# Between two attention steps: one ScalarE pass moved ahead of three projections, and block 0's products moved into an earlier period

## The chip, the cores and the metric

The kernel runs on one core of a Trainium2 chip. The metric is device time in microseconds (us) of one execution; the median of several runs is what counts. Five engines work side by side, each through its own queue in order: TensorE (PE, with its weight loads PEld), VectorE (DVE), ScalarE (ACT), GpSimd (POOL) and SyncE (SP). They meet only where one waits for another's result.

## The reference

The reference is a graph network of two layers on 2708 nodes with 256 features. Cut to what matters here:

```python
# layer 0
x = layernorm(x + relu(concat([x, adj @ x], 1) @ weight + bias))
# layer 1
R = (adj + eye(N)) / rowsum(adj + eye(N))
for n in range(2):
    q = Xa @ W1.T @ W2.T
    k = Xa @ W3.T
    probs = softmax(q @ k.T)                 # N x N
    keep = the largest probs of each row, until their sum reaches 0.9
    A = probs * keep / rowsum(probs * keep)
    Xf = R @ Xf
    Xa = A @ Xa
    Z = Z + Xf @ U1[n].T + Xa @ U2[n].T
x = layernorm(x + layernorm(x + Z))          # inner one with gain and bias
```

In each of the two steps the N x N attention is thinned in every row to the largest probabilities that hold 90% of the mass ("top-p"). `adj` has about eight entries other than zero in a row, so `R @` works on gathered rows.

## The kernel before

The 2708 rows are cut into 22 blocks of 128 (the last one, `EDGE`, has 20). All data are float32. A matmul shows as two records in the profile, a transpose as one.

Ahead of the place of interest, the kernel computes layer 0, and then step 1 of the attention block by block. At the end of a block's step 1, the result `xaT_all` (tag "V" in SBUF) is projected to the keys and queries of step 2 and, two blocks at a time, to `ya`, the right-hand side of step 2's products. `ya_pair()` does one such y pair: four matmuls into an accumulator `acc` (one of two PSUM buffers), and a copy by ScalarE (L675, for the last pair two copies L678). There are eleven pairs. The first eight run among the last instructions of step 1; the last three in a loop of their own, `while y_pairs: ya_pair()`.

Step 2 is written out by hand as a sequence of periods `per` = 0 to 23, each of six groups `g` (NG = 6). There is no scheduler: the order in which the source issues instructions is the order of each engine's queue. In a steady period four blocks are in work at once:

- block `per + 2`: TensorE makes its logits in three parts (L507, one PSUM tile `lg`, a single buffer); VectorE takes the shift from the first part (`shift`, L841); ScalarE makes the exponentials of each part (`exps2`, L844 and L848). The first part of the next block's logits is made in the last group of a period.
- block `per + 1`: ScalarE tries two levels over the whole block (`try_act`, parts 0 to 3: passes L965 and L968 of 2708 columns, and small instructions, the last of them L978 to L981 in `next_level`). The passes need an output that nobody reads, `scr`.
- block `per`: VectorE takes the last level (`last_level`, from L1002 on), makes a copy `low` of what lies below the level (`below_level`, L1022), and 20 candidates (L1029).
- block `per - 1`: VectorE sorts the candidates, finds the threshold, marks (L1082) and masks the block (`mask`, L1087). `vector_slots` is the order of the last two, six slots a period.
- block `per - 2` (`t_mul`): TensorE transposes it in six groups of four 128 x 128 tiles (`turn`, L527, PSUM tile `tr` of two buffers), ScalarE copies each group to SBUF (`wT`, two buffers, L530), and TensorE multiplies it with `ya` into an accumulator (`products`, L564), one group behind the transposes.

Beside this runs the R chain, `R @` for two right-hand sides: per block eight products ("units", `r_units`, L749) of gathered rows `yg` (POOL's indirect DMAs, L719, seven for a block, two buffers) and stored matrix tiles (SP's queue). When the eight units of a block have run, VectorE scales and adds (`r_out`, L777) two groups later. The table `units` says how many units TensorE does in each period; `first` = 16 come ahead of period 0.

The first three blocks of step 2 cannot take that form, so they have a start of their own. VectorE does both trial levels of block 0's search, except for one sum, which ScalarE makes: `try_dve(b0, 0)`, `try_dve(b0, 1)` (pass L992) on VectorE and `try_act(b0, 1, 0)` with `next_level(b0, 1)` on ScalarE. `vector_slots` has a short form for block 0 in period 1: it is sorted, marked and masked in the first four groups; block 1's last level follows in the last two.

Where tiles lie decides what may start: `tile1` (tag "x1") holds `low` and `w`, and is free once `x1` is no longer read. `tile2` (tag "V") holds the fifth buffer of the ring of blocks and `scr`; it is free once the last y pair has read `xaT_all`. POOL clears the edge of that fifth buffer (L956).

Of the kernel before, what the change touches and what calls it, by code (L numbers as in the profile page):

```python
# [9 lines left out]
FP = mybir.dt.float32  # L10
# [10 lines left out]
P = 128  # L21
# [19 lines left out]
CW, CC = 128, 7  # L41
# [107 lines left out]
def fast_path(ctx, tc, c, flags, fint, xT_d, x_d, w0_d, b0_d, w1_d, w2_d, w3_d, u1_d, u2_d, g_d, b_d):  # L149
    nc = tc.nc  # L150
    N, D, DA, NB, DC, KH, CHS, rows = c.N, c.D, c.DA, c.NB, c.DC, c.KH, c.CHS, c.rows
    ident = c.ident
    adj_d, out_d, x1_d, za_d = c.adj_d, c.out_d, c.x1_d, c.za_d
    NW = SEG * NS
    NF = flags.shape[1]

    big = ctx.enter_context(tc.tile_pool(name="big", bufs=1))
# [27 lines left out]
    b0 = es[1][:, :D]  # L185
# [44 lines left out]
    EDGE = NB - 1  # L230
# [66 lines left out]
    class Lists:  # L297
# [11 lines left out]
        def turn(self):  # L309
            n = self.n  # L310
            parts = names[:, self.a:self.b, :].rearrange("p m (s j) -> p (m s) j", j=3)
            tr = ps_tr()
            for j in range(3):
                nc.tensor.transpose(tr[:n, j, :], parts[:, :, j], ident)
            nc.scalar.copy(self.row[:n].rearrange("q (j p) -> q j p", j=3), tr[:n, :3, :])
# [72 lines left out]
    for t in range(NB):  # L388
        p = rows(t)
# [57 lines left out]
    for m in range(NB):  # L447
        p = rows(m)
# [50 lines left out]
    def logits(s, t, i):  # L499


        p = rows(t)
        lg = ps_lg()
        cs = CHS[2 * i:2 * i + 2]
        for h, (a, b) in enumerate(cs):
            o = slice(DA * h, DA * h + DA)
            nc.tensor.matmul(lg[:p, h, :b - a], lhsT=q[o, t * P:t * P + p], rhs=keys[s][o, i, :b - a],  # L507
                             start=True, stop=True)
        a, b = cs[0][0], cs[-1][1]
        return lg.rearrange("p h n -> p (h n)")[:p, :b - a], a, b  # L510
# [42 lines left out]
    def products(keep):  # L553

        if len(before) > keep:
            p, ks, wT, y, acc = before.pop(0)
            for k in ks:
                kw = rows(k)
                if p < P:
                    o = EW * (k % 4)  # L560
                    nc.tensor.matmul(acc[o:o + p, :D], lhsT=wT[:kw, k % 4, :p], rhs=y[:kw, k, :],
                                     start=k < 4, stop=k >= NB - 4)
                    continue
                nc.tensor.matmul(acc[:p, :D], lhsT=wT[:kw, k % 4, :p], rhs=y[:kw, k, :],  # L564
                                 start=k == 0, stop=k == NB - 1)
# [96 lines left out]
    def ya_pair():  # L662


        if not y_pairs:
            return
        t0 = y_pairs.pop(0)
        pz = ps_acc().rearrange("p (s d) -> p s d", d=D)
        for s in range(2):
            p, at = rows(t0 + s), (t0 + s) * P  # L670
            for j in range(DC):
                nc.tensor.matmul(pz[:p, s, :], lhsT=xaT_all[:, j, at:at + p], rhs=c.u2[:, j, 1, :],  # L672
                                 start=j == 0, stop=j == DC - 1)
        if rows(t0 + 1) == P:
            nc.scalar.copy(ya[:, t0:t0 + 2, :], pz)  # L675
            return
        for s in range(2):
            nc.scalar.copy(ya[:rows(t0 + s), t0 + s, :], pz[:rows(t0 + s), s, :])  # L678
# [129 lines left out]
    def e2(t):  # L808
        return ring[t % 5]
# [40 lines left out]
    def begin_search(b):  # L850

        nc.vector.tensor_reduce(b.z, b.all[:b.p, :NL], AX.X, ALU.add)
        yield
        nc.vector.reciprocal(b.rz, b.z)
        nc.vector.tensor_scalar(b.nz, b.z, -1.0, None, op0=ALU.mult)
        yield
        nc.vector.tensor_scalar(b.l0, b.roots, b.roots, b.rz, op0=ALU.mult, op1=ALU.mult)

    def run_all(steps):
        for _ in steps:  # L860
            pass
# [84 lines left out]
    for t in range(3):  # L946
        exps2(blocks[t], 2, *logits(1, t, 2))
        ya_pair()
    while y_pairs:
        ya_pair()  # L950

    tile1 = big.tile([P, 2 * NW], FP, tag="x1", name="w")
    low = tile1[:, :NW]
    w = tile1[:, NW:]
    tile2 = big.tile([P, 2 * NW], FP, tag="V", name="e4")
    nc.gpsimd.memset(tile2[:, N:NW], 0.0)  # L956
    ring.append(tile2[:, :NW])
    scr = tile2[:, NW:]

    def try_act(b, k, part):  # L960


        e = e2(b.t)[:b.p, :N]
        if part == 0:
            nc.scalar.activation(scr[:b.p, :N], e, AF.Relu, bias=b.nz, scale=b.l[k], accum_out=b.relu)  # L965
            return
        if part == 1:
            nc.scalar.activation(scr[:b.p, :N], e, AF.Sign, bias=b.nz, scale=b.l[k], accum_out=b.sign)  # L968
            return
        if part == 2:  # L970
            nc.scalar.activation(b.n, b.sign, AF.Identity, bias=halfn[:b.p], scale=0.5)
            return
        nc.scalar.activation(b.u[k], b.relu, AF.Identity, bias=b.n, scale=b.rz)
        next_level(b, k)

    def next_level(b, k):
        keep, slope, down = STEPS[k]
        nc.scalar.activation(b.kept, b.l[k], AF.Copy, scale=keep + TOP_P * slope, bias=-down)  # L978
        nc.scalar.activation((b.l1, b.l2)[k], b.u[k], AF.Identity, bias=b.kept, scale=-slope)
        if k:  # L980
            nc.scalar.activation(b.few, b.l1, AF.Copy, scale=TOP_P, bias=-FEW)  # L981
# [6 lines left out]
    def try_dve(b, k):  # L988

        e = e2(b.t)[:b.p, :N]  # L990
        level(b, b.l[k])
        nc.vector.scalar_tensor_tensor(w[:b.p, :N], e, b.d, e, op0=ALU.is_ge, op1=ALU.mult, accum_out=b.m)  # L992
        nc.vector.tensor_scalar(b.u[k], b.m, b.rz, b.l[k], op0=ALU.mult, op1=ALU.mult)
        if k == 0:
            keep, slope, down = STEPS[0]
            nc.vector.tensor_scalar(b.kept, b.l0, keep + TOP_P * slope, -down, op0=ALU.mult, op1=ALU.add)
            nc.vector.scalar_tensor_tensor(b.l1, b.u0, -slope, b.kept, op0=ALU.mult, op1=ALU.add)
# [251 lines left out]
    accs = {}  # L1249
# [1 line left out]

    each = NB * (CC + 1)
    first = 2 * (CC + 1)
    units = {0: CC + 1, 1: CC + 1}
    rest = each - first - sum(units.values())
    units.update({p: rest * (p - 1) // 8 - rest * (p - 2) // 8 for p in range(2, 10)})
    units.update({p: each * (p - 10) // 11 - each * (p - 11) // 11 for p in range(11, 22)})
    assert first + sum(units.values()) == 2 * each

# [1 line left out]
    b0, b1, b2 = (blocks[t] for t in range(3))  # L1261
    run_all(begin_search(b0))
    try_dve(b0, 0)
    run_all(begin_search(b1))
    try_dve(b0, 1)
    run_all(begin_search(b2))
    lg = logits(1, 3, 0)
    r_units(first)
    try_act(b0, 1, 0)
    next_level(b0, 1)  # L1270
    for per in range(NB + 2):
        if per == NB + 1:
            tail.append(True)
        n_r = units.get(per, 0)
        b_act = blocks.get(per + 1)
        t_mul = per - 2 if per > 1 else None
        if t_mul is not None:
            accs[t_mul] = ps_acc(t_mul)
        b_exp = None
        if per and per + 2 < NB:  # L1280
            b_exp = blocks[per + 2] = Block(per + 2)
        vector = vector_slots(blocks.get(per), blocks.get(per - 1), begin_search(b_exp) if b_exp else None)
        for g in range(NG):
            n = n_r * (g + 1) // NG - n_r * g // NG
            now = later.pop(0)
            later.append([])
            if g == 0:
                if b_exp:
                    shift(b_exp, lg[0])
                r_units(n)  # L1290
            if t_mul == EDGE:
                if g == 0:
                    products(0)
                    edge_product(ya, accs[EDGE], e2(EDGE))
            elif t_mul is not None:
                turn(t_mul, g, ya, accs[t_mul], e2(t_mul))
            if b_exp and g == 3:
                lg = logits(1, b_exp.t, 2)
            if g == NG - 1 and 3 < per + 3 < NB:
                lg = logits(1, per + 3, 0)  # L1300
            if g:
                r_units(n)
            if b_exp and g == 1:
                lg = logits(1, b_exp.t, 1)
            if t_mul is not None and t_mul != EDGE:
                products(1)
            if b_exp and g in (0, 1, 3):
                exps2(b_exp, (g + 1) // 2, *lg)
            if b_act:
                for k, part in {0: ((0, 0),), 1: ((0, 1), (0, 2), (0, 3)), 2: ((1, 0),), 3: ((1, 1), (1, 2), (1, 3))}.get(g, ()):  # L1310
                    try_act(b_act, k, part)
            next(vector)
            if g == 0:
                final_slot(0)
                if t_mul:
                    t = t_mul - 1
                    base = za_load(t)
                    later[0].append(lambda t=t, base=base: arrive(t, base, accs.pop(t), ras.pop(t)[:rows(t)]))
            for f in now:
                f()  # L1320
            if g and (per < NB + 1 or g < NG - 1):
                final_slot(g)
# [407 lines left out]
```

## Time and profile before

| | |
|---|---|
| median of 3 runs | 1325.51 us (1323.46 to 1327.99) |
| profiled execution | 1323.33 us, of which the span is 1321.6 us |
| TensorE (PE) | 1237.4 us busy, 94% |
| VectorE (DVE) | 1002.0 us busy, 76% |
| ScalarE (ACT) | 753.3 us busy, 57% |
| GpSimd (POOL) | 634.7 us busy, 48% |
| mean granted TensorE clock | 0.977 |
| last y pair's copy ends, step 2 begins | about 754 us into the span |

Busy time is a mean over stages with different limits. A row of a timeline gives the start in us from the start of the span, the length in us, the engine, the line and operation, output and inputs, and in brackets how long the engine had been idle before it and what ended that. A row of a table of stretches gives the stretch, its length, the busy time of each engine with the number of instructions, the granted clock, the share of the DMA engines and GB/s.

### The profile page before, as it was taken

How to read it: one execution, taken by the hardware profiler on the slowest of the kernel's cores; microseconds unless marked ns; L12 is line 12 of the kernel's file. 1: busy time of each engine (PE TensorE's matmuls, PEld its weight loads, DVE VectorE, ACT ScalarE, POOL GpSimd, SP SyncE). 2: the span in 40 equal slices, each digit the busy share in tenths (PEclk: the TensorE clock that was granted, in tenths of full speed). 3: DMA queues.
4: the chain of work that ended last, by engine and by line, in shares of the span. 5: the costliest groups of instructions: out<-in, count | busy, mean ns of one | idle time of the engine just before them, and what ended most of it. 6: DMA issues, size and time to landing. Idle time of an engine off the chain costs nothing.

```text
span 1321.6 us, 18910 instructions
## 1 busy us (share of the span) xinstructions
PE 1237.4 (94%) x5764; PEld 894.5 (68%) x5764; DVE 1002.0 (76%) x3420; ACT 753.3 (57%) x1338; POOL 634.7 (48%) x594
## 2 busy tenths in 40 slices
PE   8999999979899999999999969999999989998985
PEld 6877877833477777777775647777756766666763
DVE  2545555865999998877751399898897999899996
ACT  2010111025465556566564498878888899989931
POOL 1000000005275532677554187887847767787850
PEclk9999999989899999999998979999999999999998
DMA  7455544523222210223232155556545445544541
GB/s 191 163 173 168 167 153 142 171 67 123 92 77 82 70 62 10 76 91 99 76 77 86 55 172 179 177 178 184 172 118 159 148 128 166 173 148 146 166 108 38
DMA packets 101994, 166.28 MB, mean 126 GB/s; under 512 B 17394, under 2 KB 74358, under 8 KB 101882
## 3 DMA queue, kind: packets, MB, share of 16 engines
q1 hardware_dynamic: 75596, 108.91, 25.4%
q0 software_dynamic: 20544, 51.17, 14.1%
q10 hardware_dynamic: 5742, 4.89, 1.3%
q8 instruction: 48, 0.79, 0.2%
q14 instruction: 64, 0.52, 0.1%
HBM read 130.87 MB, written 34.03 MB: 125 GB/s over the span
## 4 chain that ended last, share of the span: by engine, by line
PE 70%; ACT 15%; DVE 11%; issue 3%; DMA 0%; ACTq 0%; DVEq 0%
PE acc L564 23%; PE acc L257 16%; PE lg L507 8%; PE tr L527 6%; PE misc L749 5%; ACT e L965 4%; ACT e L844 3%; ACT e L968 2%; DVE e L1087 2%; PE acc L651 2%; PE acc L462 2%; PE misc L426 2%; PE misc L392 2%; ACT e L848 2%; PE acc L672 2%
## 5 line engine op out<-in xcount | busy, mean ns | idle before, releaser
L530 ACT COPY wT<-tr 128x512 f32<-128x512 f32 (+2 forms) x258 | 131.8, 518 | 217.6 <-PE tr L527 215.9
L564 PE MATMUL acc<-ya,wT 128*128 128x256 f32 (+1 forms) x924 | 234.9, 394 | 11.4 <-ACT wT L530 11.0
L564 PE MATMUL acc<-x,wT 128*128 128x256 f32 (+1 forms) x924 | 230.5, 388 | 0.0
L719 POOL DMA_INDIRECT yg<-v_d,ix x154 | 195.0, 1266 | 64.6 <-issue 25.1
L564 PEld LDWEIGHTS acc<-ya,wT 128*128 128x128 f32 (+1 forms) x924 | 171.4, 194 | 66.0 <-issue 23.1
L719 POOL DMA_INDIRECT yg<-yf_d,ix x154 | 190.7, 1238 | 48.3 <-issue 24.3
L564 PEld LDWEIGHTS acc<-x,wT 128*128 128x128 f32 (+1 forms) x924 | 165.2, 189 | 71.0 <-issue 37.3
L257 PE MATMUL acc<-y,adj_t 128*128 128x257 f32 (+1 forms) x924 | 208.4, 381 | 0.0
L257 PEld LDWEIGHTS acc<-y,adj_t 128*128 128x128 f32 (+1 forms) x924 | 171.8, 189 | 32.7 <-issue 8.9
L367 POOL DMA_INDIRECT adj_t<-in_adj,ix x154 | 165.6, 1076 | 51.8 <-issue 41.7
L749 PE MATMUL misc<-yg,adj_t 128*128 128x256 f32 (+1 forms) x704 | 180.6, 392 | 5.9 <-DMA yg<-yf_d,ix 4.3
L507 PE MATMUL lg<-k,q 64*128 64x512 f32 (+3 forms) x528 | 152.4, 605 | 29.7 <-ACT e L848 22.3
L749 PEld LDWEIGHTS misc<-yg,adj_t 128*128 128x128 f32 (+1 forms) x704 | 125.2, 190 | 54.3 <-issue 23.1
L527 PE MATMUL tr<-ident,e 128*128 128x128 f32 (+2 forms) x946 | 147.9, 275 | 2.5 <-DVE e L1087 2.5
L527 PEld LDWEIGHTS tr<-ident,e 128*128 128x128 f32 (+2 forms) x946 | 114.1, 140 | 41.9 <-issue 18.8
L334 POOL DMA_DIRECT2D part_d<-e x1 | 0.6, 573 | 285.3 <-DVE e L333 285.3
L439 ACT COPY x1T<-tr 128x256 f32<-128x256 f32 (+1 forms) x22 | 8.0, 364 | 186.7 <-PE tr L438 186.7
L965 ACT ACTIVATE e<-e,st 128x2708 f32<-128x2708 f32 (+1 forms) x43 | 113.5, 2640 | 0.1
L968 ACT ACTIVATE e<-e,st 128x2708 f32<-128x2708 f32 (+1 forms) x42 | 111.0, 2642 | 0.1
L570 DVE MAX8 cand<-e 128x8 f32<-128x170 f32 (+1 forms) x352 | 87.2, 317 | 27.4 <-ACT e L514 27.4
L1029 DVE MAX8 cand<-w 128x8 f32<-128x136 f32 (+1 forms) x440 | 106.1, 285 | 0.0
L507 PEld LDWEIGHTS lg<-k,q 64*128 64x128 f32 (+1 forms) x528 | 39.5, 184 | 63.5 <-ACT e L848 30.1
(239 smaller groups left out, 1780.8 us busy)
## 6 DMA issues: line engine op xcount, KB each, us to landing
adj_t<-in_adj SPq DMA_DIRECT2D x44, 704.0 KB
adj_t<-adjc_d SPq DMA_DIRECT2D x44, 448.0 KB
adjc_d<-adj_t SPq DMA_DIRECT2D x22, 256.0 KB
base<-za_d SPq DMA_DIRECT2D x41, 128.0 KB
adjc_d<-adj_t SPq DMA_DIRECT2D x22, 192.0 KB
xt<-in_x ACTq DMA_DIRECT2D x21, 128.0 KB
x_d<-x SPq DMA_DIRECT2D x21, 128.0 KB
x1b_d<-xb SPq DMA_DIRECT2D x21, 128.0 KB
```

The source lines that it names most:

```text
L257: nc.tensor.matmul(acc[:p, :n], lhsT=halves[k // KH][:kw, k % KH, :p], rhs=y[:kw, k, :n], start=k == 0, stop=stop and k == NB - 1)
L367: nc.gpsimd.indirect_dma_start(out=a[:CW, i, :], out_offset=None, in_=adj_rows, in_offset=bass.IndirectOffsetOnAxis(ap=ix[:CW, m, i:i + 1] ...
L507: nc.tensor.matmul(lg[:p, h, :b - a], lhsT=q[o, t * P:t * P + p], rhs=keys[s][o, i, :b - a], start=True, stop=True)
L527: nc.tensor.transpose(tr[:kw, k % 4, :p], e[:p, k * P:k * P + kw], ident[:p, :p])
L530: nc.scalar.copy(wT[:, :full, :p], tr[:, :full, :p])
L564: nc.tensor.matmul(acc[:p, :D], lhsT=wT[:kw, k % 4, :p], rhs=y[:kw, k, :], start=k == 0, stop=k == NB - 1)
L570: nc.vector.max(dst[:p, i * 8:(i + 1) * 8], src[:p, i * step:i * step + w])
L719: nc.gpsimd.indirect_dma_start(out=y[:CW, i, :], out_offset=None, in_=rows_d, in_offset=bass.IndirectOffsetOnAxis(ap=ix[:CW, m, i:i + 1], ...
L749: nc.tensor.matmul(acc[:p, :D], lhsT=a[:kw, k, :p], rhs=y[:kw, k, :], start=k == 0, stop=k == CC)
L965: nc.scalar.activation(scr[:b.p, :N], e, AF.Relu, bias=b.nz, scale=b.l[k], accum_out=b.relu)
L968: nc.scalar.activation(scr[:b.p, :N], e, AF.Sign, bias=b.nz, scale=b.l[k], accum_out=b.sign)
L1029: nc.vector.max(b.cand[:p, 8 * i:8 * i + 8], low[:p, SEG2 * i:SEG2 * (i + 1)])
```

## The change

Two things are done, in one diff.

First, `try_act(b0, 1, 0)`, ScalarE's pass over block 0, is issued right after VectorE's first trial and ahead of the last three y pairs. As `tile2` isn't there yet at that place, its unread output goes to `low` (`spill_room`); `tile2` is made after the pairs, and later passes write there as before. `next_level(b0, 1)` comes right after VectorE's second trial.

Second, block 0's transposes and products move from period 2 to the last two groups of period 1, three `turn`s in each, with `products(1)` after each `turn`. Period 2 has none then; the table of R units is rewritten: 20 units in period 2, and what is left is spread over periods 3 to 9 (17 or 18 each) instead of 18 in each of periods 2 to 9. The output of block 0's attention is taken in period 3 as before.

```diff
-    while y_pairs:
-        ya_pair()
 
     tile1 = big.tile([P, 2 * NW], FP, tag="x1", name="w")
     low = tile1[:, :NW]
     w = tile1[:, NW:]
-    tile2 = big.tile([P, 2 * NW], FP, tag="V", name="e4")
-    nc.gpsimd.memset(tile2[:, N:NW], 0.0)
-    ring.append(tile2[:, :NW])
-    scr = tile2[:, NW:]
+    spill_room = [low]
 
     def try_act(b, k, part):
         e = e2(b.t)[:b.p, :N]
+        scr = spill_room[0]
...
-    units = {0: CC + 1, 1: CC + 1}
+    units = {0: CC + 1, 1: CC + 1, 2: 20}
     rest = each - first - sum(units.values())
-    units.update({p: rest * (p - 1) // 8 - rest * (p - 2) // 8 for p in range(2, 10)})
+    units.update({p: rest * (p - 2) // 7 - rest * (p - 3) // 7 for p in range(3, 10)})
...
     run_all(begin_search(b0))
     try_dve(b0, 0)
+    try_act(b0, 1, 0)
+    while y_pairs:
+        ya_pair()
     run_all(begin_search(b1))
     try_dve(b0, 1)
+    next_level(b0, 1)
     run_all(begin_search(b2))
+    tile2 = big.tile([P, 2 * NW], FP, tag="V", name="e4")
+    nc.gpsimd.memset(tile2[:, N:NW], 0.0)
+    ring.append(tile2[:, :NW])
+    spill_room[0] = tile2[:, NW:]
     lg = logits(1, 3, 0)
     r_units(first)
-    try_act(b0, 1, 0)
-    next_level(b0, 1)
     for per in range(NB + 2):
...
-        t_mul = per - 2 if per > 1 else None
+        t_mul = 0 if per == 1 else per - 2 if per > 2 else None
...
-            elif t_mul is not None:
+            elif t_mul:
                 turn(t_mul, g, ya, accs[t_mul], e2(t_mul))
             if b_exp and g == 3:
                 lg = logits(1, b_exp.t, 2)
+            if t_mul == 0 and g > 3:
+                for i in range(3):
+                    turn(0, 3 * (g - 4) + i, ya, accs[0], e2(0))
+                    products(1)
             if g == NG - 1 and 3 < per + 3 < NB:
                 lg = logits(1, per + 3, 0)
             if g:
                 r_units(n)
...
-            if t_mul is not None and t_mul != EDGE:
+            if t_mul and t_mul != EDGE:
                 products(1)
```

## The prediction

> **What bounds the kernel now.** I read the page first (shares, then the chain that ended last), then a table of stretches around the seam between the steps, then the timeline of that seam. The page:
>
> ```profile
> PE 1237.4 (94%) x5764; PEld 894.5 (68%) x5764; DVE 1002.0 (76%) x3420; ACT 753.3 (57%) x1338; POOL 634.7 (48%) x594
> ...
> PE 70%; ACT 15%; DVE 11%; issue 3%; DMA 0%; ACTq 0%; DVEq 0%
> ```
>
> TensorE is busy 94% of 1321.6 us and carries 70% of the chain. So only stretches where it is not full can be filled. The table of stretches (us, then busy time of PE, PEld, DVE, ACT, POOL, the granted clock, DMA) shows them:
>
> ```profile
> 754.00:762.00 8.00, 7.89 (x36) 6.00 (x32) 4.28 (x9) 7.93 (x10) 5.40 (x5) 1.00 0.42 120
> 762.00:770.00 8.00, 3.41 (x11) 2.05 (x12) 7.72 (x36) 7.79 (x11) 6.18 (x7) 0.92 0.82 254
> 770.00:778.00 8.00, 7.69 (x22) 4.28 (x21) 7.69 (x27) 7.90 (x14) 5.86 (x8) 0.65 0.57 159
> 778.00:784.60 6.60, 1.51 (x6) 0.68 (x4) 6.43 (x10) 6.47 (x11) 5.99 (x3) 0.83 0.37 131
> 784.60:790.20 5.60, 5.52 (x15) 3.39 (x16) 5.53 (x31) 3.82 (x8) 4.38 (x5) 0.59 0.30 88
> ...
> 814.30:838.45 24.15, 23.84 (x115) 17.97 (x114) 21.04 (x78) 19.92 (x33) 19.28 (x16) 1.00 0.55 169
> ```
>
> From 762 to 784.6 VectorE and ScalarE are full, while TensorE works 3.41 of 8, 7.69 of 8 (at 0.65 of its clock) and 1.51 of 6.6 us. From 814.3 it works 23.84 of 24.15 us in each period of step 2: from there TensorE sets the pace. The seam ends when block 1's transposes (the first work of period 3) start, at 814.29. The timeline of all engines (start, length, instruction, idle time ahead and its releaser) for the start of the seam:
>
> ```profile
> 748.48 0.59 ACT L675 COPY ya<-acc 128x512 f32<-128x512 f32 x1 [1.00 <-PE acc L672]
> 754.30 2.65 ACT L965 ACTIVATE e<-e,st 128x2708 f32<-128x2708 f32 x1
> ```
>
> ScalarE copies y pairs (L675) and begins block 0's pass (L965) only at 754.30. Then:
>
> ```profile
> 757.58 0.22 DVE L1002 SCALAR_TENSOR_TENSOR st<-st 128x1 f32<-128x1 f32 x1 [6.32 <-ACT st L981]
> ...
> 761.76 0.87 DVE L777 SCALAR_TENSOR_TENSOR base<-misc,rinv,base 128x256 f32<-128x256 f32 x2
> ...
> 774.17 1.79 PE L507 MATMUL lg<-k,q 64*128 64x512 f32 x4
> ...
> 777.32 3.05 DVE L1087 SCALAR_TENSOR_TENSOR e<-w,st,e 128x2720 f32<-128x2720 f32 x1
> ...
> 784.68 2.08 PE L507 MATMUL lg<-k,q 64*128 64x512 f32 x4 [5.17 <-ACT e L844]
> ...
> 788.33 0.19 ACT L981 ACTIVATE st<-st 128x1 f32<-128x1 f32 x1
> ```
>
> VectorE sat idle 6.32 us for ScalarE's trial (757.58), ran the two R outputs L777 at 761.76, finished masking block 0 (L1087) at 777.32 + 2.97 + 0.08 = 780.4; ScalarE's last small step of block 2's trials ends at 788.52, and it had no gap since 754.30. VectorE alone from there:
>
> ```profile
> 789.38 0.28 DVE L841 TENSOR_REDUCE nmax<-lg 128x1 f32<-128x128 f32 x1
> ...
> 807.62 3.04 DVE L1087 SCALAR_TENSOR_TENSOR e<-w,st,e 128x2720 f32<-128x2720 f32 x1
> ...
> 830.50 0.15 DVE L852 TENSOR_REDUCE bulk<-st 128x1 f32<-128x3 f32 x1 [3.00 <-ACT e L844]
> ```
>
> Its period 2 begins with the shift (L841) at 789.38 and masks block 1 at 807.62 + 3.04 = 810.7, so TensorE takes block 1 3.6 us after VectorE has it. The first row is the one this change touches: the shift reads block 4's logits, which TensorE made at 784.68.
>
> **Part 1, ScalarE's pass over block 0 ahead of the last three y pairs.** It needs l1 of the first trial on VectorE (L997, done at 746.25 + 0.16 = 746.4) and ScalarE free of the copy at 748.48 + 0.59 = 749.07. It runs 749.07 to 751.8, 5.2 us earlier. Behind it stand three pairs' copies. The first moves from 750.20 to 751.8-752.4, and TensorE's last pair, which needs that accumulator (two buffers), starts at 752.4 instead of 751.9: +0.5. Behind this pair stand block 3's logits and the first 16 R products (32 records, 754.72 to 761.89), which now end at about 762.4. The small steps L978 to L981 also wait for the second trial (750.6) and end at about 755.4 instead of 757.55: 2.1 us won.
>
> What is late next? On VectorE the pass below the level then ends at 759.7, but the next instruction is L777 twice, and the second needs R product 16, at 762.4. Before, the pair ran at 761.76 without a wait. So the 20 candidates begin at 762.9 instead of 762.55: VectorE loses 0.35 and the 2.1 are gone. On ScalarE the lead lasts until block 3's second logits (774.17 for 1.79 us). They are queued behind two R products that wait for gathers, and the gathers wait for R products that are 0.5 later (0.35 after a VectorE pass of 3.05 us has moved off one of them). So logits end at 776.3, ScalarE goes on at 776.35 instead of 776.07, and finishes block 2 at 788.8 instead of 788.52. Part 1 alone: -0.3 us, practically nothing.
>
> **Part 2, block 0's transposes and products in period 1.** In the changed order TensorE has, in groups 4 and 5 of period 1, eight transposes, then product groups and the other transposes with one R product between, and only after them block 4's first logits. Nothing is added or removed; 22 transposes and 22 products change place, with R products going the other way (20 in period 2 instead of 18).
>
> The transposes wait for the mask of block 0: 780.7. Two groups fit in the two transpose buffers, then the first product needs its copy wT on ScalarE. The six copies now stand behind the whole of block 2's trials, so the first one runs at 788.8 + 0.58 = 789.4. From there TensorE needs, by the rows of later periods: products 1.92 + 4 x 1.73 = 8.84, transposes 3 x 0.44 + 0.22 = 1.54, one R product of two records 0.43, logits 1.1: 11.9, to 801.3 at full clock. (Copies of 0.58 hide behind products of 1.73; without that cover six of them cost 3.5.) TensorE will have idled 8 us before, and what that does is seen in the rows after the 5.17 us of idle time here:
>
> ```profile
> 784.68 2.08 PE L507 MATMUL lg<-k,q 64*128 64x512 f32 x4 [5.17 <-ACT e L844]
> 786.69 3.65 PE L749 MATMUL misc<-yg,adj_t 128*128 128x256 f32 x10
> ...
> 814.29 0.60 PE L527 MATMUL tr<-ident,e 128*128 128x128 f32 x4
> ```
>
> The logits took 2.08 instead of the 1.13 that the same four records take at 793.97 (+0.95), the ten R records 3.65 instead of 10 x 0.2165 (+1.48), at a granted clock of 0.59: a restart costs 2.4 us. I take that, so the logits of block 4 end at 803.7 instead of 786.76.
>
> The Trainium skill, "TensorE: Matmul & The Clock Gate", section "Part 1: The HAM clock gate", says that the clock halves after an idle window of about 3.4 us and comes back after about 3.4 us of work. By that the restart would cost 1.7 us, and my forecast would be 0.7 lower; the rule speaks against letting TensorE wait inside block 0.
>
> Queued behind those logits: the shift of block 4 on VectorE, and behind it everything of period 2 (blocks 1 and 2); on ScalarE block 4's exponentials and behind them block 3's trials. VectorE reaches the shift at 789.4 + 0.35 = 789.75 and idles until 803.7: 14 us. From shift to the end of the mask it took 810.7 - 789.4 = 21.3, with 0.67 of waiting that will be covered: 20.6. So block 1 is masked at 824.3. TensorE has no other work by then: 54 R products are done and logits 5 wait only for ScalarE (803.7 + 0.3 for the shift, 12.7 from its first to its third exponential, which are 791.29 and 805.39 before, less three copies of 0.47 that fall away, and 0.9 for the third itself: 817.6). It starts block 1 at 824.4 instead of 814.29: 10.1 late, with 54 R products behind it instead of 53, worth 0.43. Sum: +9.7 us.
>
> From there the order is that of before; every period has 23.84 busy of 24.15, so the loss stays. The R products are the same in total by period 9.
>
> Costed at nothing: the memset of the fifth buffer's edge and another one change place on POOL (0.11 each); on SP one load and one store of the R chain swap; block 0's accumulator is taken a period earlier (two buffers, one used). Block 5's last gather waits for R products now behind block 0, at about 804 instead of 797.57. Gathers took up to 4.4 us to be usable at this place (ended 765.15, product at 769.60), so 809.4 against a need at about 812. If that cover is gone it costs up to 2 us.
>
> **Bounds.** Least: ScalarE keeps its lead (-2.1) and the restart runs at full clock (-2.4): +5.2. Most: a second slow restart at 824 (+2.4) and the gathers (+2): +14. I take +9.7, nearest to the rows; a second restart is less likely since R products run until shortly before 824.
>
> The profiled execution took 1323.33 us (1321.6 span and 1.7 around it), the median is 1325.51: 2.2 above it. The forecast is 1333.0 for such an execution and 1325.51 + 9.7 = 1335.2 for the median.
>
> **Rivals.** (a) Milder: lead kept and full clock, +5.2, 1330.7. For it: the gather waits are scattered (1.49, 2.16, 0.65 us); against it: TensorE is idle 8 us in any case. (b) Faster: block 0 fills TensorE's idle time and VectorE sees no new wait. Then block 1 is masked at 810.4 (810.7 + 0.35 - 0.67), TensorE starts it there instead of at 814.29 and is 0.43 ahead: -4.3, 1321.2. It decides at block 4's logits: ready by 789.75 they cost nothing, by 794 the gain is gone, and each us later is a us lost. For it: TensorE idles from 779.5 to 784.68. Against: ScalarE's trials run without a gap to 788, and 10.8 us of TensorE's work stand between the first copy and the logits. (c) No change: the loss is given back in later periods, 1325.5. For it: VectorE waits 3.00 us in period 3 (830.50 above). Against: TensorE, which has 0.3 us a period to spare, takes no part. That the change isn't done as described is excluded by the instruction order.
>
> **How the numbers follow.** Forecast 0.72, (a) 0.14, (b) 0.08, (c) 0.06. A change of 0.3% (4 us) is about what a measurement can tell; forecast and (a) both lie above it. The likeliest time is 1335.2. The forecast's own bounds with (a) give 1330.7 to 1339.5; 1.7 us less at the low end for the spread of the times before: 1329.0 to 1339.5.
>
> **What would show it.** Right: ScalarE's pass over block 0 near 749; VectorE's R outputs still ending after 762; the first copy of block 0 near 789; VectorE idle over 10 us ahead of the shift of block 4, released by TensorE's logits; block 1's transposes near 824, then periods of 24.1 us. Wrong: that shift before 795, copies of block 0 before 786, or later periods clearly shorter than 24 us.

## The result: 8.6 us slower, lost in the seam

| | before | after |
|---|---|---|
| median, us (7 runs each) | 1325.51 (1323.46 to 1327.99) | 1334.06 (1330.81 to 1334.92) |
| ratio of after to before | | 1.0058, 95% interval 1.0044 to 1.0072 |
| profiled execution, us (its span) | 1323.33 (1321.6) | 1334.06 (1332.3) |

By the interval the loss is 5.8 to 9.5 us. In the code after, lines from 961 on have numbers 4 lower than before (L965 is L961, L981 is L977, L1087 is L1083). The page of the kernel after, busy time and chain:

```profile
PE 1240.0 (93%) x5764; PEld 894.5 (67%) x5764; DVE 1001.6 (75%) x3420; ACT 753.3 (57%) x1338; POOL 637.7 (48%) x594
...
PE 68%; ACT 15%; DVE 11%; issue 3%; DMA 2%; SPq 0%; ACTq 0%; DVEq 0%
```

The page hardly moves: the work is the same, only the span is longer. The table of stretches of the kernel after (stretch, length, busy time of PE, PEld, DVE, ACT, POOL with instructions, granted clock, DMA share, GB/s) shows where:

```profile
778.00:789.00 11.00, 3.51 (x18) 1.70 (x16) 10.76 (x27) 10.84 (x15) 9.17 (x7) 0.76 0.38 120
789.00:806.00 17.00, 15.31 (x69) 12.30 (x70) 3.85 (x24) 5.65 (x16) 7.30 (x8) 0.86 0.22 63
806.00:826.00 20.00, 16.62 (x59) 10.42 (x57) 19.86 (x72) 16.16 (x24) 16.04 (x14) 0.83 0.61 184
826.00:850.00 24.00, 23.98 (x115) 17.91 (x114) 23.89 (x89) 19.75 (x34) 19.43 (x16) 1.00 0.59 178
```

In the second row TensorE is full and the others are nearly empty, VectorE with 3.85 of 17 us. The first row is the opposite: TensorE has 3.51 of 11 us. The two do not overlap. From 826 on, periods are as full as before. The timeline of the kernel after, row by row (start, length, instruction, idle time ahead and its releaser):

```profile
749.73 0.59 ACT L675 COPY ya<-acc 128x512 f32<-128x512 f32 x1 [1.00 <-PE acc L672]
750.21 2.65 ACT L961 ACTIVATE w<-e,st 128x2708 f32<-128x2708 f32 x1
...
763.78 0.48 DVE L777 SCALAR_TENSOR_TENSOR base<-misc,rinv,base 128x256 f32<-128x256 f32 x1 [2.32 <-PE misc L749]
...
777.72 1.11 ACT L844 ACTIVATE e<-lg,nmax 128x1024 f32<-128x1024 f32 x1 [2.46 <-PE lg L507]
...
782.07 1.09 PE L527 MATMUL tr<-ident,e 128*128 128x128 f32 x8 [1.34 <-DVE e L1083]
...
790.07 1.05 ACT L530 COPY wT<-tr 128x512 f32<-128x512 f32 x2
...
803.04 1.13 PE L507 MATMUL lg<-k,q 64*128 64x512 f32 x4
804.22 0.29 DVE L841 TENSOR_REDUCE nmax<-lg 128x1 f32<-128x128 f32 x1 [13.12 <-PE lg L507]
...
825.10 0.60 PE L527 MATMUL tr<-ident,e 128*128 128x128 f32 x4
```

The pass over block 0 runs directly behind the copy at 749.73. What it wins is given back to R product 16 (VectorE, 2.32 us at 763.78) and to block 3's second logits (ScalarE, 2.46 us at 777.72). The transposes of block 0 come with its mask (782.07), the copies only behind block 2's trials (790.07). Block 4's logits end at 804.17, and VectorE has waited 13.12 us for them.

The copy at 749.73 lies 1.25 us later than before (748.48). No edit touches anything ahead of it, and in the runs below it lies between 748.1 and 750.5; so from here on I count from the start of this copy, the "mark". Block 1's transposes start 75.37 us behind it, against 65.81 before: **9.56 us lost in the seam.**

The later way, as the difference to before of the start of VectorE's mask of a block: block 2 +9.56, blocks 5 to 9 +9.07, block 10 and all later ones +7.37. So 1.70 come back between blocks 9 and 10 (23.28 us instead of 24.97; before, TensorE's clock drops in that period, after it doesn't). And 2.1 go at the very end, where the edge block's 22 transposes (L544) and 44 records of products (L550) run. The timeline of TensorE there, of the kernel before and then of the kernel after:

```profile
1302.95 3.30 PE L550 MATMUL acc<-ya,wT 128*20 128x256 f32 x44 [0.65 <-ACT wT L546]
```

```profile
1311.13 5.74 PE L550 MATMUL acc<-ya,wT 128*20 128x256 f32 x44 [0.65 <-ACT wT L546]
```

The sum for the two profiled executions is 1.25 + 7.37 + 2.1 = 10.7 us. This is the whole difference of their spans. Of it 1.25 belongs to the run and not to the change.

### The profile page after: what moved, and what is told of

Its sections match the earlier page's. It is cut to its first block, busy times and chain, and to the rows that moved or that the text cites. A ratio compares the mean times of both kernels' runs of the same rounds, so it can differ in the third digit from the quotient of the medians.

```text
span 1332.3 us, 18912 instructions
## 1 busy us (share of the span) xinstructions
PE 1240.0 (93%) x5764; PEld 894.5 (67%) x5764; DVE 1001.6 (75%) x3420; ACT 753.3 (57%) x1338; POOL 637.7 (48%) x594
## 4 chain that ended last, share of the span: by engine, by line
PE 68%; ACT 15%; DVE 11%; issue 3%; DMA 2%; SPq 0%; ACTq 0%; DVEq 0%
PE acc L564 23%; PE acc L257 15%; PE lg L507 8%; PE tr L527 6%; PE misc L749 6%; ACT e L961 3%; ACT e L844 3%; ACT e L964 2%; DVE e L1083 2%; PE acc L651 2%; PE acc L462 2%; PE misc L426 2%; PE misc L699 1%; ACT wT L530 1%; ACT e L848 1%
## 5 line engine op out<-in xcount | busy, mean ns | idle before, releaser
L719 POOL DMA_INDIRECT yg<-v_d,ix x154 | 195.0, 1266 | 62.9 <-issue 25.2
L719 POOL DMA_INDIRECT yg<-yf_d,ix x154 | 191.3, 1242 | 55.9 <-issue 24.7
L507 PE MATMUL lg<-k,q 64*128 64x512 f32 (+3 forms) x528 | 151.3, 601 | 25.6 <-ACT e L848 20.5
L964 ACT ACTIVATE e<-e,st 128x2708 f32<-128x2708 f32 (+1 forms) x42 | 110.9, 2641 | 0.1
L961 ACT ACTIVATE e<-e,st 128x2708 f32<-128x2708 f32 (+1 forms) x42 | 110.9, 2640 | 0.1
```

What stands on the lines that cost most here:

```text
L719: nc.gpsimd.indirect_dma_start(out=y[:CW, i, :], out_offset=None, in_=rows_d, in_offset=bass.IndirectOffsetOnAxis(ap=ix[:CW, m, i:i + 1], ...
```

## The experiments

### Each part alone

`e1_part1` is the kernel before with the first part of the change (the pass and `next_level` moved, `spill_room`); `e2_part2` is the kernel before with the second (block 0 in period 1, the new table of R units). Of the change's diff they hold these lines, and what belongs to them:

```diff
 # e1_part1
+    try_act(b0, 1, 0)
+    while y_pairs:
+        ya_pair()
     run_all(begin_search(b1))
...
 # e2_part2
+    units = {0: CC + 1, 1: CC + 1, 2: 20}
+        t_mul = 0 if per == 1 else per - 2 if per > 2 else None
+            if t_mul == 0 and g > 3:
+                for i in range(3):
+                    turn(0, 3 * (g - 4) + i, ya, accs[0], e2(0))
+                    products(1)
```

> Part 1 alone: ScalarE's pass over block 0 ahead of the last three y pairs; block 0's transposes and products and the table of R products as before. Queue theory (block 4's first logits stand behind block 0's products and hold VectorE 13 us; this is the whole loss): 1325.5 within 1.5 us, VectorE's shift of block 4 without a wait. Rival 'pairs' (the pass ahead of the pairs is what costs, since the last y pair, block 3's logits and the first 16 R products come later): 1330 or more. Third possibility, part 1 does what it is for: ScalarE 2 us earlier carries through, 1323.5.

> Part 2 alone: block 0's transposes and products in period 1 and the new table of R products; ScalarE's pass over block 0 after the y pairs as before. Queue theory: all of the loss, 1334 within 1.5 us, VectorE waits 12 to 14 us ahead of the shift of block 4. Rival 'pairs': under 1328.

Part 1: median 1324.81 us, ratio 0.9993 (0.9979 to 1.0008). Part 2: 1333.21 us, 1.0051 (1.0034 to 1.0069). The timeline of VectorE with part 1 alone, then with part 2 alone:

```profile
764.14 0.48 DVE L777 SCALAR_TENSOR_TENSOR base<-misc,rinv,base 128x256 f32<-128x256 f32 x1 [2.32 <-PE misc L749]
...
791.37 0.28 DVE L841 TENSOR_REDUCE nmax<-lg 128x1 f32<-128x128 f32 x1
```

```profile
803.21 0.29 DVE L841 TENSOR_REDUCE nmax<-lg 128x1 f32<-128x128 f32 x1 [13.29 <-PE lg L507]
```

The whole loss is part 2. Part 1 has the wait for the R product, and its masks from block 1 on come 0.2 to 0.56 us earlier; no time that can be measured. But its way is not that of the whole change. The timeline of ScalarE and TensorE with part 1 alone:

```profile
776.43 1.11 ACT L844 ACTIVATE e<-lg,nmax 128x1024 f32<-128x1024 f32 x1 [0.80 <-PE lg L507]
...
787.05 4.34 PE L749 MATMUL misc<-yg,adj_t 128*128 128x256 f32 x10
```

ScalarE waits only 0.80 us for block 3's second logits (2.46 in the kernel after) and ends block 2's trials 38.8 us behind the mark, 1.25 us earlier than before; in the kernel after it ends them 0.4 us later than before. Of the 1.25 us TensorE loses 0.69, since its ten R records after the idle time take 4.34 us instead of 3.65.

### Which instruction holds VectorE

`e3_logits_first` is the whole change, with block 4's first logits ahead of block 0's transposes:

```diff
+            if per == 1 and g == 4:
+                lg = logits(1, per + 3, 0)
             if t_mul == 0 and g > 3:
                 for i in range(3):
                     turn(0, 3 * (g - 4) + i, ya, accs[0], e2(0))
                     products(1)
-            if g == NG - 1 and 3 < per + 3 < NB:
+            if g == NG - 1 and 4 < per + 3 < NB:
```

> The whole change, but block 4's first logits ahead of block 0's transposes in period 1. VectorE's shift of block 4 then has no wait (13.1 us in the changed kernel). If this wait alone is the loss: 1321 to 1326. But ScalarE's exponentials of block 4 still stand behind the six copies of block 0, which TensorE's products pace until about 802; VectorE takes block 4's sums between the marks of block 1 (L852) and would wait there until about 803 + 14 = 817 instead of 806, then one mark and the mask pass: block 1 masked near 822 instead of 824.7. So, if what counts is the place of both on the two queues: 1331, and a wait of about 10 us at L852 takes the place of that at the shift.

Median 1330.05 us, ratio 1.0033 (1.0019 to 1.0046). The timeline of VectorE:

```profile
791.54 0.28 DVE L841 TENSOR_REDUCE nmax<-lg 128x1 f32<-128x128 f32 x1
...
803.21 0.48 DVE L777 SCALAR_TENSOR_TENSOR base<-misc,rinv,base 128x256 f32<-128x256 f32 x1 [5.84 <-PE misc L749]
```

The wait ahead of the shift is gone. The time is close to the expected 1331, but the wait is mostly not where I had put it: VectorE waits 5.84 us for an R product (above), and 1.76 at L852, where I had expected 10. The wait of 2.32 us that belongs to part 1 is there too, as in the kernel after. The R products stand behind block 0's products on TensorE as well. So it isn't the one instruction: whatever is queued on TensorE behind a block whose copies come late is late too. In the seam 6.2 us stay lost (mask of block 2) instead of 9.56.

### The price of the restart

`e4_busy` is the whole change with 14 matmuls that nobody reads, between the second `turn` of block 0 and its first product:

```diff
                 for i in range(3):
                     turn(0, 3 * (g - 4) + i, ya, accs[0], e2(0))
+                    if (g, i) == (4, 1):
+                        for _ in range(14):
+                            nc.tensor.matmul(accs[0][:, :D], lhsT=ident, rhs=ya[:, 0, :], start=True, stop=True)
                     products(1)
```

> The whole change, and 14 matmuls of 128x256 into block 0's accumulator, ahead of its first product, whose result nobody reads: TensorE is busy in the 7.5 us in which it waits for ScalarE's copies. If the first product group took 3.55 us instead of 1.92 because TensorE had been idle (granted clock 0.5), it takes 1.9 now and block 4's logits come about 1.6 us earlier. If the slow group has another reason, it stays at 3.5. In time up to 1.6 us less than the changed kernel, or no difference.

One run: 1330.79 us. TensorE's timeline of this kernel:

```profile
782.32 6.91 PE L1306 MATMUL acc<-ya,ident 128*128 128x256 f32 x28
789.07 1.89 PE L564 MATMUL acc<-ya,wT 128*128 128x256 f32 x8
```

Block 0's first product group takes 1.89 us instead of 3.55 in the kernel after, the shift waits 11.36 us instead of 13.12, and block 2's mask is 1.8 us earlier than after. So 1.7 to 1.8 of the loss are the half clock. The other 7.8 stay with this order of the queue; the next section changes the order.

Why 1.6 here and 2.4 in the kernel before? The records of the granted clock tell when it was 0.50. A table of stretches that each cover one such drop, the first row from the kernel before, the others from the kernel after:

```profile
782.37:789.20 6.83, 4.52 (x10) 2.57 (x11) 6.76 (x26) 6.05 (x11) 5.61 (x5) 0.50 0.25 75
...
783.63:793.87 10.24, 3.18 (x8) 2.53 (x9) 7.40 (x26) 7.39 (x13) 8.11 (x8) 0.50 0.31 87
...
817.76:824.59 6.83, 6.30 (x14) 3.99 (x15) 6.83 (x13) 4.27 (x9) 5.61 (x5) 0.50 0.68 183
```

TensorE worked 4.52, 3.18 and 6.30 us of these drops. Half of that is 2.3, 1.6 and 3.2 us, and the rows show 2.4, 1.6 and 3.05 us lost (the last from 2.08 and 4.96 us, which take 1.13 and 2.86 at full clock). So here a restart costs half of the time that TensorE works in the drop, and not a fixed price: the longest drop was the cheapest, as TensorE came back near its end.

### A smaller move: two groups only

The prediction had said that block 0's work is free in period 1 as long as block 4's logits are ready when VectorE wants them. Two kernels move only two of the six groups and leave the rest in period 2. `e5_two_turns`, from before (the other four `turn`s go to groups 0 to 3 of period 2):

```diff
             if g == NG - 1 and 3 < per + 3 < NB:
                 lg = logits(1, per + 3, 0)
+            if per == 1 and g == NG - 1:
+                accs[0] = ps_acc(0)
+                turn(0, 0, ya, accs[0], e2(0))
+                turn(0, 1, ya, accs[0], e2(0))
```

`e7_two_groups` puts the two `turn`s into group 3, behind the mask of block 0 and ahead of ScalarE's last pass over block 2 (L968), and block 4's logits with block 0's first product into group 4:

```diff
+            if per == 1 and g == 4:
+                lg = logits(1, per + 3, 0)
+                products(1)
...
+            if per == 1 and g == 3:
+                next(vector)
+                accs[0] = ps_acc(0)
+                turn(0, 0, ya, accs[0], e2(0))
+                turn(0, 1, ya, accs[0], e2(0))
             if b_act:
```

> The order of before, with a small share of the move: only the first two of block 0's six groups of transposes and copies stand at the end of period 1, behind block 4's first logits; the other four, and all of its products, are in period 2. Theory (what was lost was the wait of block 4's logits behind block 0, not the use of TensorE's time in period 1 as such): no wait ahead of the shift of block 4 (it starts within 0.5 us of where it would start by VectorE's own work), and block 1's transposes come up to 2.3 us earlier relative to the 8th y pair's copy, since 0.9 us of transposes and up to 1.5 us of waiting for a copy leave the path; time 1323 to 1325.5. Rival (ScalarE is the bound at this place, whatever stands on TensorE): two copies of 0.5 us ahead of block 4's exponentials push these and block 3's trials back, block 1's transposes come 0 to 1 us later, time 1325.5 to 1326.5.

> The order of before, with two groups of block 0's transposes and their copies ahead of ScalarE's last pass over block 2, so that the copies do not stand behind all of block 2's trials; then block 4's first logits (a group earlier), then block 0's first product; the other four groups and all other products in period 2. Theory (the prediction's condition: free as long as block 4's logits are there when VectorE has ended block 0, about 789.75): the copies run near 785 instead of 790, no wait of over 1 us ahead of the shift of block 4, block 1's transposes up to 3.3 us earlier relative to the 8th y pair's copy (VectorE's mask of block 1 then sets the end), time 1322 to 1324.5. Rival (ScalarE has no room there): the copies wait for TensorE's transposes behind the mask of block 0 and hold back ScalarE's last pass over block 2 by 1 to 2 us, VectorE waits for that pass's sums, and block 1's mask and transposes come 0 to 2 us later: time 1325.5 to 1327.5.

Medians 1323.99 and 1324.52 us beside 1325.01 of before; both ratios 0.9992 (0.9983 to 1.0000, and 0.9984 to 1.0001). Neither waits ahead of the shift, and block 1's transposes come 1.04 and 1.42 us earlier. So the condition holds, and the mechanism of the loss with it. But the gain is less than half of the most that was expected (2.3 and 3.3). The timeline of ScalarE and VectorE with two groups:

```profile
785.74 1.06 ACT L530 COPY wT<-tr 128x512 f32<-128x512 f32 x2
...
794.12 0.59 ACT L530 COPY wT<-tr 128x512 f32<-128x512 f32 x1 [3.44 <-PE tr L527]
...
809.46 0.15 DVE L852 TENSOR_REDUCE bulk<-st 128x1 f32<-128x3 f32 x1 [2.83 <-ACT e L844]
```

The copies run at 785.74 as expected. But the third group's copy stands ahead of block 4's exponentials on ScalarE, and its transposes behind twelve R records on TensorE: 3.44 us, which come out as 2.83 at L852.

### Pushing the seam as far as it goes

`e9_three_busy` mends this (from two groups): the third `turn` right behind the first product, and 14 unread matmuls ahead of the logits against the half clock. `e10_three_busy_part1` adds part 1. In `e11_three_seven` and `e12_three_seven_part1` these are 7 matmuls, the only difference.

```diff
             if per == 1 and g == 4:
+                for _ in range(14):
+                    nc.tensor.matmul(accs[0][:, :D], lhsT=ident, rhs=ya[:, 0, :], start=True, stop=True)
                 lg = logits(1, per + 3, 0)
                 products(1)
+                turn(0, 2, ya, accs[0], e2(0))
```

> As the kernel with two groups, with two more edits: 14 unread matmuls ahead of block 4's first logits hold the clock up, and the third group of transposes of block 0 goes right behind its first product, ahead of the R products, so that its copy does not hold ScalarE 3.4 us ahead of block 4's exponentials. Theory: logits 1.1 us and first product 1.9 instead of 2.08 and 3.17, the exponentials of block 4 at about 791 instead of 794.6, the wait of 2.83 us ahead of L852 gone, block 1's transposes 2.3 to 2.9 us earlier than before, relative to the 8th y pair's copy (with two groups: 1.4); time 1322 to 1324. Rival (TensorE waits for ScalarE again at block 4's second logits, as before, and takes the gain back): 0.5 to 1.5 us earlier, time 1324 to 1325.

> The same with part 1 (ScalarE's pass over block 0 ahead of the last three y pairs). Part 1 alone moved the masks 0.4 to 0.56 us forward. Theory: the gains add, block 1's transposes 2.7 to 3.4 us earlier than before, time 1321.5 to 1323.5. Rival (ScalarE's order is only shifted): the same within 0.3 us as without part 1.

> As the kernel with three groups, with 7 unread matmuls instead of 14: each had cost two records of 0.22 us, so 14 took 6.21 us and held block 4's logits until 789.53, 2.6 us longer than ScalarE did. Theory: with 3.1 us they end before ScalarE lets the logits go, TensorE is 2.6 us earlier from there on, and block 1's transposes start 3.5 to 3.9 us earlier than before, relative to the 8th y pair's copy (with 14: 1.3); time 1321.3 to 1323. Rival (VectorE or ScalarE take over as the last ones of the seam): 1.5 to 2.5 us earlier, a wait behind VectorE's mask or ScalarE's third exponentials; time 1323 to 1324.

> The same with part 1. Theory (VectorE's mask of block 1 is now the limit, and part 1 moves it 0.4 us forward): block 1's transposes 3.9 to 4.3 us earlier than before, relative to the 8th y pair's copy, time 1321 to 1322.7. Rival (TensorE's own work is the limit, part 1 is worth nothing): as without part 1, within 0.2 us.

| | median | ratio (95%) | block 1's transposes | mask of block 9 |
|---|---|---|---|---|
| e9 | 1324.54 | 0.9991 (0.9979 to 1.0003) | -1.32 | +0.74 |
| e10 | 1323.73 | 0.9994 (0.9983 to 1.0004) | -0.95 | +1.40 |
| e11 | 1324.80 | 0.9997 (0.9986 to 1.0008) | -3.71 | +0.16 |
| e12 | 1323.73 | 0.9991 (0.9981 to 1.0001) | -3.86 | -1.01 |

The two last columns are differences to before, from the mark. My 14 matmuls were too many (two records each, 6.21 us); with 7 the seam is 3.7 us shorter, as theory had it. And the time is unchanged as far as can be measured. TensorE's timeline of `e11_three_seven`, in the seam and two periods later:

```profile
785.42 1.13 PE L507 MATMUL lg<-k,q 64*128 64x512 f32 x4 [0.56 <-ACT e L844]
...
810.88 0.60 PE L527 MATMUL tr<-ident,e 128*128 128x128 f32 x4
...
862.73 0.70 PE L749 MATMUL misc<-yg,adj_t 128*128 128x256 f32 x2 [0.64 <-DMA yg<-yf_d,ix]
864.60 1.22 PE L749 MATMUL misc<-yg,adj_t 128*128 128x256 f32 x2 [1.17 <-DMA yg<-yf_d,ix]
865.75 2.08 PE L507 MATMUL lg<-k,q 64*128 64x512 f32 x4
```

TensorE waits for gathered rows, then runs at half clock (granted 0.50 in 865.75 to 867.76), and from block 3's transposes to block 4's it takes 27.75 us instead of 24.17. The lead is gone in this one period.

The gathers come from POOL (L719). The page gives POOL 48%, and 19.65 of 24.22 us busy in the period from 856.03. But it issues them without a pause: 0.95 us and 0.30 to the next one, 1.25 in all, and two in a period are stretched to 3.5 to 3.8 us while VectorE has a pass of 3.05. Thirteen of 1.25 and two of about 4.0 are 24.2 us: **POOL is as full as TensorE.** In the kernel before its stream has no gap above 0.31 us from 755.69 to 972.87. POOL's timeline, the end of this stream in the kernel before, and then two rows of the kernel after:

```profile
971.92 0.95 POOL L719 DMA_INDIRECT yg<-yf_d,ix  x1 [0.30 <-PE misc L749]
988.69 0.95 POOL L719 DMA_INDIRECT yg<-v_d,ix  x1 [15.82 <-PE lg L507]
```

```profile
797.11 0.94 POOL L719 DMA_INDIRECT yg<-yf_d,ix  x1 [1.16 <-PE misc L749]
805.08 0.94 POOL L719 DMA_INDIRECT yg<-yf_d,ix  x1 [7.02 <-PE misc L749]
```

After the change POOL starts 0.60 us later and stands 8.2 us in the two places shown, for R products that are behind block 0. All kernels, as differences to before, from the mark:

| | mask of block 2 (seam) | end of POOL's stream | mask of block 9 |
|---|---|---|---|
| after | +9.56 | +9.05 | +9.06 |
| e2 | +9.39 | +8.98 | +8.98 |
| e4 | +7.78 | +7.24 | +7.27 |
| e3 | +6.20 | +3.32 | +5.77 |
| e8 (below) | +2.79 | -0.97 | +2.80 |
| e1 | -0.56 | -0.53 | -0.23 |
| e5 | -0.57 | +0.01 | +0.38 |
| e7 | -0.95 | +1.82 | +1.24 |
| e13 (below) | -1.54 | +1.33 | +0.89 |
| e9 | -1.37 | +1.35 | +0.74 |
| e10 | -1.00 | +1.39 | +1.40 |
| e11 | -3.71 | +0.04 | +0.16 |
| e12 | -3.45 | -1.00 | -1.01 |

Block 9 follows the later of the two, the seam or POOL, within 0.7 us. No kernel ends POOL's stream more than about 1.0 us earlier than before, and no shorter seam has won more than that at block 9. A longer seam loses nearly all of it. TensorE's waits agree: from 830 to 985 us it waits for gathered rows in all seven kernels with a shorter seam (`e5`, `e7`, `e9` to `e13`), 0.7 to 2.1 us in sum, and never in the kernels before and after, `e2`, `e3`, `e4` and `e8`.

Why POOL's stream ends earlier or later in kernels where it never waits can be read from its rows. In each kernel 18 of its 140 gathers are stretched, and all of them begin inside one of VectorE's passes of 3.05 us. Each ends 0.81 to 0.83 us behind the end of that pass. Two rows of the kernel before:

```profile
855.95 3.04 DVE L1087 SCALAR_TENSOR_TENSOR e<-w,st,e 128x2720 f32<-128x2720 f32 x1
856.03 3.78 POOL L719 DMA_INDIRECT yg<-yf_d,ix  x1 [0.30 <-issue]
```

So a gather that begins early in a pass is long, and one that begins late is short (in five kernels one that begins in the first 0.03 us of a pass is not stretched). The 18 take 59.5 us before, 61.3 in `e7` (whose stream ends 1.82 later) and 57.7 in `e12` (which starts 0.60 later with part 1 and ends 1.0 earlier).

### The half clock in the kernel before

`e8_before_busy` is the kernel before with 20 unread matmuls in TensorE's idle time ahead of block 4's logits, in group 5 of period 1; `e13_before_ten` has 10.

```diff
+            if per == 1 and g == NG - 1:
+                accs[0] = ps_acc(0)
+                for _ in range(20):
+                    nc.tensor.matmul(accs[0][:, :D], lhsT=ident, rhs=ya[:, 0, :], start=True, stop=True)
             if g == NG - 1 and 3 < per + 3 < NB:
                 lg = logits(1, per + 3, 0)
```

> The kernel before with 20 matmuls (128x256, result overwritten unread) in TensorE's idle time ahead of block 4's first logits, so that the clock does not drop there. Theory (the half clock after 5.17 us of idle time is not on the path in the kernel before, since TensorE waits again for ScalarE at block 4's second logits, 1.47 us): the logits take 1.1 us instead of 2.08 and the ten R products 2.2 instead of 3.65, TensorE's wait ahead of the second logits grows from 1.5 to about 3.9 us, and block 1's transposes start within 0.5 us of before, relative to the 8th y pair's copy. Rival (the half clock is part of what the seam costs before): block 1's transposes come 2 to 2.4 us earlier.

> The kernel before with 10 unread matmuls (4.3 us) instead of 20 (10.4 us in two stretches of records, which held block 4's logits until 791.6) in TensorE's idle time ahead of block 4's logits. Theory (half clock off the path in the kernel before): logits 1.1 us instead of 2.08, R products 2.2 to 2.4 instead of 3.65, TensorE's wait ahead of block 4's second logits 1 to 4 us, block 1's transposes within 0.5 us of before, relative to the 8th y pair's copy. Rival (half clock on the path, since block 0's first copy waits for transposes that stand behind the slow R products): the first copy and the exponentials of block 4 come 2.4 us earlier, and with them block 1's transposes 1.5 to 2.4 us.

Twenty overran: logits at 791.62, VectorE waits 1.35 us for them, the mask of block 2 comes 2.79 us later (1328.21, one run). Ten fit, and their run (1323.63) goes against my theory: the first copy of block 0 comes 1.5 us earlier than before and block 1's transposes too (64.27 behind the mark, against 65.81). TensorE's wait at block 4's second logits (1.47 in all three kernels) is a wait for ScalarE, which itself had waited for the transposes behind the slow R products. A wait ahead of an instruction does not show that what ran earlier is off the path. This gain, too, is gone by block 9 (+0.89).

## Why the prediction was right

The forecast was +9.7 us; the medians are 8.55 apart, and the forecast lies just above the interval of 5.8 to 9.5.

**Part 1** went as worked out within the whole change: the pass at the copy's end, the 2.1 us lost to R product 16 and the lead lost at block 3's second logits. That its forecast of -0.3 fits the -0.2 to -0.56 of part 1 alone is luck: the terms ahead of it made things 0.28 to 0.35 later, not earlier, and in `e1_part1` ScalarE kept 1.25 us of the lead.

**The first copy behind block 2's trials:** done at 789.4 by the forecast, 40.9 behind the mark; the first product starts at 790.69, 41.0 behind it.

**The wait of the shift:** 14 us forecast, 13.12 measured. The term that was off is the restart, taken as 2.4. The first product group took 3.55 instead of 1.92, which is 1.63 us: TensorE came back 3.18 us ahead of the end of the drop, and in my row 4.52 us ahead of it. The estimate of 1.7 by the Trainium skill ("TensorE: Matmul & The Clock Gate", "Part 1: The HAM clock gate") was nearer here than my row, but not at the second restart, which cost 3.05.

**From shift to mask, and TensorE's start:** 20.6 forecast, measured from 804.22 to 821.71 + 3.04: 20.5. Block 1's transposes: +10.1 forecast, +9.56 measured; the restart took 0.77 less than forecast, and 0.25 came on top by what follows. **The second restart**, held to be less likely, did come: at 818.29 TensorE's logits take 2.08 us and the next 12 records 4.96. It cost only some 0.25 us, since VectorE's mask of block 1 ended at 824.75 anyway.

**The R product ahead:** 0.43 forecast; the step from +9.49 to +9.07 between the masks of blocks 4 and 5 is 0.42.

**"The loss stays"** holds to block 9. Then 1.7 come back and 2.1 are lost at the end, both by where the clock drops. The half clock at the end is in `e2`, `e4`, `e5`, `e9` and `e12` as well and not in `e1`, `e3`, `e7`, `e8`, `e10`, `e11` and `e13`, one profiled execution of each; since `e3`, the change with one item in another place, lacks it, I don't put it down to the change.

**The gathers, costed at nothing,** are the step that failed without showing in the sum. Their place was right (55.5 behind the mark, measured 55.35), but I took 797.57 to 804 as slack. It was none: POOL's standing makes up some 7.6 of the 9.05 us by which its stream ends later. The seam is late by as much, so the loss is that of one of them and not of both. How much the late gathers would cost with a seam that is on time is not separated by these runs.

**Rival (b)** was refused for the right reason: logits at 55 behind the mark instead of 41. Its price was wrong. I had -4.3 from TensorE and VectorE alone; `e11_three_seven` reaches -3.7 in the seam, and the time is 0.9997 of before. In rival (c) the argument named TensorE's 0.3 us to spare in a period; POOL, which has none either, is missing from it.

No version here is shown to beat the kernel before: the six smaller moves (`e5`, `e7`, `e9` to `e12`) have medians 0.2 to 1.2 us below it, and every interval reaches 1. All of them beat the kernel after.

## What to carry to other kernels

Before work is moved into an engine's idle time, look for when its inputs are ready on the engine that makes them last, and then at what is queued behind it in order: eight idle us are worth nothing to work whose copies come at their end, and everything behind it pays. Keep the first item of the next stage ahead of it, and move only the part whose inputs are there. Before a gain is put down, look at every engine for a stream without gaps: one that is 80% busy in a period, with a fixed pause before each instruction, can be as full as one at 99%, and then, as here, losses count and gains do not.

## What was unexpected in the hardware

- **Gathers on POOL have a pitch.** 0.95 us each, 0.30 between them, never less in this stretch; beside VectorE's passes of 3.05 us one takes up to 3.79, as it ends some 0.8 us behind the pass in which it began.
- **The clock drops after short waits too.** In `e11_three_seven` two waits of 0.64 and 1.17 us (TensorE busy 1.85 of 3.02 us) were followed by logits of 2.08 us at a granted clock of 0.50; in the kernel after, a wait of 2.81 us was followed by such logits and twelve records that took 4.96 us instead of 2.86. The idle window of about 3.4 us in the Trainium skill ("TensorE: Matmul & The Clock Gate", "Part 1: The HAM clock gate") is a longer pause than either; here the traces decide.
- **Where it drops shifts with the phase.** The period between the masks of blocks 9 and 10 takes 24.97 us in the kernel before and 23.28 after, and the products of the edge block 3.30 or 5.74, without an edit at either place: some 2 us each, as much as most of the edits tried here. The short period is also in `e2`, `e3`, `e4`, `e7`, `e10`, `e12` and `e13`, so that `e12`, by the masks 1.0 us ahead at block 9, is 2.7 ahead from block 10 on; then it has the slow end (5.49). In the fourteen traces a drop lasts 3.41, 6.83 or 10.24 us (the one that runs past the end of the program apart), and those of one trace begin whole numbers of 3.41 us apart. A wait of 1.88 us in the kernel before (ahead of 1003.57) met such a drop, and one of 1.89 us at the same place of `e12` did not.
